# A softmax's sums over keys by one-column products, its output banks added on GpSimd, and a renewed plan, in an attention and state-space kernel

## The chip, the cores and the metric

The kernel runs on one core of one Trainium2 chip, as one program. The metric is the device time of one execution in microseconds (us). Three executions give the time before; a fourth, profiled execution gives the trace. An instruction's engine is named as in the profile: PE is TensorE's matmul, PEld its weight load, DVE is VectorE, ACT is ScalarE, POOL is GpSimd, SP is SyncE, which here only issues DMAs.

## The reference, cut to what matters

A block of a model: layer norm, eight-head cross-attention from 4096 queries to 3202 keys (head width 64), a second layer norm, a state-space scan, and two residual additions, all in float32.

```python
x = _layernorm(builder_state, g1, beta1)          # 4096 x 512
base_n = _layernorm(base_state, g1, beta1)        # 3202 x 512
# _mha: 8 heads of 64
scores = jnp.einsum('bhqd,bhkd->bhqk', q, k) * (1.0 / np.sqrt(HD))
attn = jax.nn.softmax(scores, axis=-1)
out = jnp.einsum('bhqk,bhkd->bhqd', attn, v)
...
x = residual + out @ W_o.T + b_o
xn = _layernorm(x, g2, beta2)
U = (xn @ W_in.T + b_in) @ Bmat
def step(s, u_t):                                 # a scan over the 4096 rows
    s = jax.nn.silu(s @ A.T) + u_t
    return (s, s)
...
return residual + states @ Cmat + mod
```

The change is in the softmax: its denominators (the sums over the keys), the join of the attention output before it is divided by them, and the order in which all pieces of the attention stage stand.

## The kernel before, in words

**Stages.** The first 300 us or so load and normalise the keys and make keys and values in DRAM. The attention stage follows, up to about 2400 us; the state-space scan and the last rows close the program.

**A unit.** The attention is 64 units: one pair of heads (`hp`, four pairs) by 256 queries (`QU`). A unit has 13 steps (`NDC`), each of two chunks of about 123 keys. Keys lie on the partitions, queries along the free axis, so a step's tile is 123 partitions by 2 heads by 2 chunks by 256 queries, 1024 elements to a partition.

- `scores` (L616): eight products of 64x64 weights with 256 columns into a PSUM tile `s` (two buffers).
- `keep` (L630): ACT copies `s` into an SBUF tile `p`. `running` (the pieces `top`, L645): DVE keeps the largest score over the steps; the last step takes three half-size instructions (L639 to L641).
- `spread` (L653), `maximum` (L660), `everywhere` (L668): PE transposes the running maximum, DVE reduces it over the keys, PE spreads the result over the key partitions into the PSUM tile `mb`.
- `subtract` (the pieces `less`, L676): DVE takes the maximum from each kept tile; `weights` (L686): ACT makes the exponentials in place.
- `product` (L705): PE multiplies values by weights into `po`, two PSUM banks, one for each half of the keys. `add` (L694): POOL adds the 13 weight tiles into `acc`, 12 additions of 1024 elements.
- `output` (L735): ACT copies bank 0 of `po` to `o`. `join` (L739): DVE adds bank 1.
- `finish`: `both` (L749), POOL adds the two chunk halves of `acc`, 512 elements; `turn` (L755), PE transposes the result in four pieces into `pd`; `inverse` (L763, L764), DVE sums `pd` over the keys and takes the reciprocal; `wide` (L768), ACT repeats it; `back` (L773), PE transposes it back; `scale` (L781), DVE multiplies `o` by it.

Between these come the pieces of other rows: the next 512 queries' layer norm and heads (`queries`, `heads` L302), and for finished rows the output projection (L902), `x1` (L912), the second layer norm and the scan's inputs (`project`; on POOL `row` L896, `mod` L916 and `factors` L819 to L821).

**Order.** Nothing on the chip picks the order: each engine executes its instructions as written. A class `Plan` writes them. Each piece has an engine, a cost in ns, the pieces it must follow, a due time, and the buffers it takes and gives back. `order` plays the engines forward in time and gives each free engine the ready piece that is due first. `SHIFT` moves the due times of a sort of piece; `LATE` is the delay from a piece's end to the start of one that waits for it; `START` and `AGAIN` are added to the cost of a `scores` or `product` piece on PE, `AGAIN` where the piece before it on PE was one of these too; `RUN` and `ALONE` say how far PE should keep to one of the two kinds. Costs in the plan are of the plan alone: they set an order, not a time. PSUM has one buffer `m` in this stage, which `spread`, `turn`, `back`, the heads, the projection and the transposes take in turn.

Of the kernel before, what the change touches and what calls it, by code (L numbers as in the profile page):

```python
# [10 lines left out]
F32 = mybir.dt.float32  # L11
# [42 lines left out]
class Plan:  # L54
# [7 lines left out]
    LATE = {"PE": 110, "DVE": 130, "ACT": 110, "POOL": 100, "SP": 3000}  # L62
    START, AGAIN = 200, 10
    RUN = 1
    ALONE = dict(scores=300, product=1300)

    SHIFT = {
        "back": -2600, "both": -1300, "everywhere": -2600, "heads": 2000, "heads2": -5800,
        "maximum": 18900, "output": -1300, "product": 1300, "query.copy": -300,
        "query.spread": -3200, "query.turn": 1200, "row.inputs": -1300, "row.mean": 2000,  # L70
        "row.mod": 8100, "row.row": 6500, "row.spread": -1300, "row.turn": 2300, "row.x1": 2600,
        "scores": -300, "spread": 600, "turn": -1900, "weights": 1300,
    }
# [91 lines left out]
def xattn_ssm_kernel(  # L165
# [565 lines left out]
    def output(w):  # L731
        Q, hp, half = w["at"]
        o = op.tile([P, QU], F32, tag="o", name=f"o_{Q}_{hp}_{half}", bufs=12)
        o_t[Q, hp, half] = o
        nc.scalar.copy(o, w["po"][:, 0, :QU])  # L735

    def join(w):
        o = o_t[w["at"]]
        nc.vector.tensor_tensor(o, o, w["po"][:, 1, :QU], ALU.add)  # L739

    def finish(w, i, d, plan):

        name = w["name"]
        at_ = w["at"]

        def both():
            acc = w["acc"]
            w["both"] = accp.tile([CK, 2, QU], F32, tag="both", name=f"both_{name}", bufs=1)
            nc.gpsimd.tensor_tensor(w["both"], acc[:, :, 0, :], acc[:, :, 1, :], ALU.add)  # L749

        def turn():
            w["pd"] = m_tile([P, 2, 2, CK], f"pd_{name}")
            for t in range(2):
                for a in range(2):
                    nc.tensor.transpose(  # L755
                        w["pd"][:, t, a, :],
                        w["both"][:, a, t * P : (t + 1) * P],
                        ident[:CK, :CK],
                    )

        def inverse():
            w["rd"] = small.tile([P, 2, 2], F32, tag="rd", name=f"rd_{name}")
            nc.vector.tensor_reduce(w["rd"], w["pd"], AX.X, ALU.add)  # L763
            nc.vector.reciprocal(w["rd"], w["rd"])  # L764

        def wide():
            w["wide"] = op.tile([P, 2, 2, HD], F32, tag="rd", name=f"wide_{name}", bufs=1)
            nc.scalar.copy(w["wide"], w["rd"].unsqueeze(3).to_broadcast([P, 2, 2, HD]))  # L768

        def back():  # L770
            w["rb"] = m_tile([P, 512], f"rb_{name}")
            for t in range(2):
                nc.tensor.transpose(  # L773
                    w["rb"][:, t * P : (t + 1) * P],
                    w["wide"][:, t].rearrange("p a d -> p (a d)"),
                    ident,
                )

        def scale():
            o = o_t[at_]  # L780
            nc.vector.tensor_tensor(o, o, w["rb"][:, :QU], ALU.mult)  # L781

        plan.add(("both", i), "POOL", 1280, both, [("add", i, NDC - 1)], d - STEP,
                 ["both"], [("acc", ("add", i, 1))])
        plan.add(("turn", i), "PE", 600, turn, [("both", i)], d + 3000,
                 ["m"], [("both", ("both", i))])
        plan.add(("inverse", i), "DVE", 850, inverse, [("turn", i)], d + 5000,
                 ["rd"], [("m", ("turn", i))])
        plan.add(("wide", i), "ACT", 400, wide, [("inverse", i)], d + 6000,
                 ["wide"], [("rd", ("inverse", i))])  # L790
        plan.add(("back", i), "PE", 350, back, [("wide", i)], d + 7000,
                 ["m"], [("wide", ("wide", i))])
        plan.add(("scale", i), "DVE", 390, scale, [("back", i), ("join", i)], d + 8000,
                 [], [("m", ("back", i))])
# [5 lines left out]
    def norm_pieces(plan, k, get, d, after, name, give):  # L800
# [26 lines left out]

        plan.add((*k, "mean"), "ACT", 820, mean_, after, d, ["nm", "xh"])
        plan.add((*k, "spread"), "ACT", 820, spread_, [(*k, "mean")], d + 1000, ["sq"])
        plan.add((*k, "factors"), "POOL", 1050, factors_, [(*k, "spread")], d + 2000,  # L830
# [5 lines left out]
    def queries(plan, Q, d):  # L836

        xns, copied = [], []
        for t in range(NT):
# [12 lines left out]
            def turn(t=t, nv=nv, r=r, v=v):  # L852
                if t % 2 == 0:
# [7 lines left out]
                     ["m", "xn"] if t % 2 == 0 else ["m"], [("xh", (*k, "mean"))])  # L861
            plan.add((*k, "copy"), "ACT", 600, lambda v=v: next(v["turn"], None),
                     [(*k, "turn")], d + 5 * STEP, [], [("m", (*k, "turn"))])
# [5 lines left out]
    def head_pieces(plan, Q, hps, xns, copied, d, apart, xn_):  # L869
        for hp in hps:  # L870
            v = {}

            def head(v=v, hp=hp):
                v["heads"] = heads(Q, hp, xns)
                next(v["heads"])

            plan.add(("heads", Q, hp), "PE", 1850, head, copied, d, ["m", "q"], xn_)
            plan.add(("heads2", Q, hp), "PE", 1850, lambda v=v: next(v["heads"]),
                     [("heads", Q, hp)], d + 1, [], xn_)
            plan.add(("q", Q, hp), "ACT", 680, lambda v=v: next(v["heads"], None),  # L880
                     [("heads2", Q, hp)], d + STEP, [], [("m", ("heads", Q, hp))])
            d += apart

    def project(plan, Q, tiles, d, index):

        for t in tiles:
# [31 lines left out]
            def store(v=v, r=r):  # L918
# [3 lines left out]
            plan.add((*k, "load"), "SP", 60, load, [from_(d - 4 * STEP)], d - 4 * STEP, ["x"])  # L922
            plan.add((*k, "row"), "POOL", 1280, row, [(*k, "load")], d - STEP)
            o_ = [("o_", ("output", i)) for i in units_]
            plan.add((*k, "outs"), "PE", 1850, partial(outs, 0),
# [5 lines left out]
                             ("x1", (*k, "outs")))  # L931
            plan.add((*k, "mod"), "POOL", 1280, mod, [(*k, "x1")], d + 2 * STEP, [],
                     [("x1", (*k, "outs"))])
# [21 lines left out]
            def kept(v=v, hs=hs, c0=c0):  # L955
# [9 lines left out]
                     [("xh", (*k, "mean"))])  # L965
            plan.add((*k, "copy"), "ACT", 600, copy, [(*k, "turn")], d + 6 * STEP, [],
                     [("m", (*k, "turn"))])
# [230 lines left out]
    def last_unit(plan, w, n, d):  # L1198
# [3 lines left out]
        def copied():  # L1202
            o_t[w["at"]] = op.tile([P, QU], F32, tag="o", name=f"o_{w['name']}", bufs=12)
            nc.scalar.copy(o_t[w["at"]], w["po"][:, 0, :QU])

        def summed():
            sums(w["pd"], w["acc"], CK, False, True)
# [13 lines left out]
        plan.add("l.copied", "ACT", 370, copied, [("product", n, NDC - 1)], d, ["o_"])  # L1221
        plan.add("l.join", "DVE", 400, partial(join, w), ["l.copied"], d)
        plan.add("l.summed", "PE", 860, summed,
# [138 lines left out]
    def unit(plan, i):  # L1362
# [20 lines left out]
        for c in range(NDC):  # L1383
# [3 lines left out]
                     [("q", ("heads", Q, hp))], "scores")  # L1387
            plan.add(("keep", i, c), "ACT", 990, partial(keep, w, c), [("scores", i, c)], d + 1000,
                     ["p"], [("s", ("scores", i, c))])
            if c:  # L1390
                plan.add(("top", i, c), "DVE", 1145 if c < NDC - 1 else 2000, partial(running, w, c),
                         [("keep", i, c), ("top" if c > 1 else "keep", i, c - 1)], d + 2000,
# [3 lines left out]
                 [("top", ("top", i, 1))])  # L1396
        plan.add(("maximum", i), "DVE", 665, partial(maximum, w), [("spread", i)], d + 1000,
                 ["max"], [("m", ("spread", i))])
# [3 lines left out]
        for c in range(NDC):  # L1402
            d = (s0 + c + NDC + LAG) * STEP
            plan.add(("less", i, c), "DVE", 1145, partial(subtract, w, c), [("everywhere", i)], d,
                     [], [("b", ("everywhere", i))])
            plan.add(("weights", i, c), "ACT", 1050, partial(weights, w, c), [("less", i, c)],
                     d + 1200)
# [10 lines left out]
            elif c:  # L1418
                plan.add(("add", i, c), "POOL", 2380, partial(add, w, c),
                         [("weights", i, c), ("weights" if c == 1 else "add", i, before)], d + 2400,  # L1420
# [5 lines left out]
        if not w["last"]:  # L1426
            plan.add(("output", i), "ACT", 400, partial(output, w), [("product", i, NDC - 1)], d,
                     ["o_"])
            plan.add(("join", i), "DVE", 400, partial(join, w), [("output", i)], d + 500, [],
                     [("o", ("product", i, 0))])  # L1430
            finish(w, i, d, plan)
# [91 lines left out]
    with tc.manual_schedule():  # L1523
        for g in range(AHEAD):
            load_k(*steps[g])
        plan = Plan(
            dict(
                s=2, m=1, b=1, o=1, p=NDC + LAG + 4, top=2, acc=2, both=1, q=6, x=3, x1=2, xn2=1,
                xn=2, rstd=2, nm=2, sq=2, xh=2, max=2, rd=2, wide=1, o_=12,
# [113 lines left out]
```

## Time and profile before

| what | value |
|---|---|
| median of three runs | 2483.82 us (2482.64 to 2487.72) |
| profiled execution, its own time | 2485.21 us |
| its span in the trace | 2483.4 us |
| granted TensorE clock, mean over the span | 0.993 of full speed |
| busy share of the span: PE, DVE, ACT, POOL | 92%, 85%, 77%, 83% |
| busy in the stretch 500 to 2300 us: PE, DVE, ACT, POOL | 1699.1, 1711.6, 1556.7, 1713.4 us of 1800 |

The shares over the whole span mix the stages: up to 300 us DVE, ACT and POOL have little to do. The stretch from 500 to 2300 us holds nothing but attention units. A group of instructions in the profile is given as line, engine, operation, output and inputs, count, busy time and mean duration, then the idle time of the engine just before these instructions with what ended it. An engine starts its next instruction a little before or after the end of the last, so durations of neighbours overlap or leave gaps; the distance from one start to the next is what an instruction takes up.

### The profile page before, as it was taken

To read this page: it belongs to the slowest core of one execution; us is meant where nothing else is said; L and a number is where in the kernel's file an instruction comes from. 1 tells how busy PE (TensorE), PEld (TensorE's weight loads), DVE (VectorE), ACT (ScalarE), POOL (GpSimd) and SP (SyncE) were. 2 spreads that over 40 slices of the span, in tenths; PEclk is the share of its full clock that TensorE was granted. 3 is DMA by queue.
4 is the path that set the end of the run, shared out by engine and by line. 5 is a ranking of instruction groups with operands and counts; after the bars stand their busy time and mean duration, and the time that the engine had idled before them with its cause. 6 is when DMAs were issued, how large, how long until landed. Compare 5 with 4: busy or idle time off the path is not lost.

```text
span 2483.4 us, 70816 instructions
## 1 busy us (share of the span) xinstructions
PE 2296.9 (92%) x29718; PEld 1355.7 (55%) x29718; DVE 2108.2 (85%) x2307; ACT 1917.3 (77%) x2373; POOL 2071.5 (83%) x1197
## 2 busy tenths in 40 slices
PE   7999888999999999999999999999998999999987
PEld 3444545555555555655565555555565556555544
DVE  2111599999999999999999999999999999999975
ACT  2223588888987899788988988789978998888852
POOL 1111199989998999989998999899999999899984
PEclk9999999999999999999999999999999999999998
DMA  3432322122211222122211221222212221234364
GB/s 119 129 101 82 89 63 61 35 65 66 73 53 55 67 68 69 51 72 78 66 49 51 68 71 54 56 67 75 61 52 66 78 69 51 80 116 124 107 170 149
DMA packets 178140, 190.92 MB, mean 77 GB/s; under 512 B 14252, under 2 KB 151256, under 8 KB 177818
## 3 DMA queue, kind: packets, MB, share of 16 engines
q1 hardware_dynamic: 173270, 178.67, 24.3%
q10 hardware_dynamic: 4548, 7.67, 1.0%
q8 instruction: 237, 3.88, 0.7%
q14 instruction: 85, 0.70, 0.1%
HBM read 156.40 MB, written 29.89 MB: 75 GB/s over the span
## 4 chain that ended last, share of the span: by engine, by line
PE 44%; DVE 21%; POOL 13%; issue 10%; ACT 8%; DMA 2%; SPq 1%; ACTq 0%; POOLq 0%; DVEq 0%
PE s L616 13%; PE po L705 12%; POOL acc L694 12%; DVE top L645 12%; DVE p L676 6%; PE pq L302 5%; ACT p L630 4%; ACT p L686 3%; PE pv L543 3%; PE pk L569 3%; PE pa L902 1%; PE mb L668 1%; PE tt L653 1%; PE pd L755 1%; DMA x<-in_x_dram 1%
## 5 line engine op out<-in xcount | busy, mean ns | idle before, releaser
L694 POOL TENSOR_TENSOR acc<-p,acc 122x1024 f32<-122x1024 f32 x701 | 1660.3, 2369 | 64.1 <-ACT p L686 26.2
L676 DVE TENSOR_TENSOR p<-p,mb 123x1024 f32<-123x1024 f32 (+2 forms) x832 | 996.2, 1210 | 27.8 <-PE mb L668 27.8
L630 ACT COPY p<-s 123x1024 f32<-123x1024 f32 (+2 forms) x832 | 837.0, 1009 | 206.8 <-PE s L616 178.6
L616 PE MATMUL s<-q,k 64*64 64x256 f32 (+3 forms) x13312 | 884.9, 384 | 90.9 <-DVE top L645 79.9
L686 ACT ACTIVATE p<-p 123x1024 f32<-123x1024 f32 (+2 forms) x832 | 874.8, 1061 | 80.8 <-DVE p L676 77.3
L705 PE MATMUL po<-p,v 64*64 64x256 f32 (+3 forms) x13312 | 857.3, 379 | 26.9 <-ACT p L686 25.1
L645 DVE TENSOR_TENSOR top<-s,top 123x1024 f32<-123x1024 f32 (+1 forms) x640 | 777.4, 1215 | 11.8 <-ACT p L630 11.3
L616 PEld LDWEIGHTS s<-q,k 64*64 64x64 f32 (+3 forms) x13312 | 448.2, 130 | 428.6 <-DVE top L645 154.5
L705 PEld LDWEIGHTS po<-p,v 64*64 64x64 f32 (+3 forms) x13312 | 489.8, 133 | 268.4 <-ACT p L686 70.0
L694 POOL TENSOR_TENSOR acc<-p,p 124x1024 f32<-124x1024 f32 x64 | 152.3, 2380 | 94.2 <-DMA k<-kd 73.0
L242 POOL TENSOR_SCALAR ve_c<-mv_c 123x1 f32<-123x1 f32 (+2 forms) x26 | 6.0, 232 | 147.7 <-DVE mv_c L235 118.6
L302 PE MATMUL pq<-xn,wq 128*128 128x256 f32 x512 | 127.2, 392 | 0.0
L902 PE MATMUL pa<-wo,o 128*128 128x512 f32 x240 | 119.0, 618 | 0.0
L513 DVE COPY ct<-tp_c 128x492 f32<-128x492 f32 (+2 forms) x13 | 8.7, 671 | 125.1 <-PE tp_c L270 125.1
L302 PEld LDWEIGHTS pq<-xn,wq 128*128 128x128 f32 x512 | 92.2, 189 | 34.3 <-issue 23.6
L577 ACT ACTIVATE ks<-pk,bias 128x492 f32<-128x492 f32 (+3 forms) x28 | 18.0, 643 | 120.0 <-PE pk L569 58.1
L645 DVE TENSOR_TENSOR top<-s,p 124x1024 f32<-124x1024 f32 x64 | 78.0, 1219 | 37.8 <-DMA k<-kd 31.8
L543 PE MATMUL pv<-wv,ct 128*123 128x512 f32 (+2 forms) x208 | 98.8, 620 | 0.0
L660 DVE TENSOR_REDUCE m<-tt 128x4 f32<-128x496 f32 x64 | 42.9, 671 | 58.8 <-PE tt L653 58.8
L569 PE MATMUL pk<-ct,wk 128*128 128x492 f32 (+3 forms) x224 | 89.1, 550 | 0.0
L749 POOL TENSOR_TENSOR both<-acc 124x512 f32<-124x512 f32 x63 | 81.2, 1289 | 2.0
L902 PEld LDWEIGHTS pa<-wo,o 128*128 128x128 f32 x240 | 40.6, 189 | 51.9 <-issue 50.8
(196 smaller groups left out, 1514.3 us busy)
## 6 DMA issues: line engine op xcount, KB each, us to landing
k<-kd SPq DMA_DIRECT2D x324, 123.0 KB
v<-vd SPq DMA_DIRECT2D x324, 123.0 KB
k<-kd SPq DMA_DIRECT2D x108, 124.0 KB
v<-vd SPq DMA_DIRECT2D x108, 124.0 KB
xr<-in_x_dram SPq DMA_DIRECT2D x32, 256.0 KB
x1d<-xr SPq DMA_DIRECT2D x32, 256.0 KB
x<-in_x_dram SPq DMA_DIRECT2D x28, 256.0 KB
cx<-in_ctx_dram SPq DMA_DIRECT2D x18, 246.0 KB
```

The costliest lines, as they stand in the source:

```text
L302: nc.tensor.matmul(pq[:, half * QU : (half + 1) * QU], wq[:, i, hp * P : (hp + 1) * P], xns[half][:, i, :], start=(i == 0), stop=(i == NC ...
L543: nc.tensor.matmul(pv[:n, :H], ct[:, i, o : o + n], wv[:, i, :], start=(i == 0), stop=(i == NC - 1),)
L569: nc.tensor.matmul(pk[:, :n_g], wk[:, i, hp * P : (hp + 1) * P], ct[:, i, :n_g], start=(i == 0), stop=(i == NC - 1),)
L616: nc.tensor.matmul(s[k0:k1, a, b, :], kts[(*w["at"][:2], c)][r, b * n + k0 : b * n + k1], q[r], start=True, stop=True, skip_group_check=True,)
L630: nc.scalar.copy(t[:n], w["ps"][c][:n])
L645: nc.vector.tensor_tensor(w["top"][:n], s[:n], before[:n], ALU.max)
L676: nc.vector.tensor_tensor(t[:n], t[:n], w["mb"][:n].unsqueeze(2).to_broadcast([n, 2, 2, QU]), ALU.subtract,)
L686: nc.scalar.activation(t[:n], t[:n], AF.Exp)
L694: nc.gpsimd.tensor_tensor(w["acc"][:n], t[:n], before[:n], ALU.add)
L705: nc.tensor.matmul(w["po"][a * HD : (a + 1) * HD, k, :QU], vts[(*w["at"][:2], c)][k0:k1, b, a * HD : (a + 1) * HD], t[k0:k1, a, b, :], sta ...
L749: nc.gpsimd.tensor_tensor(w["both"], acc[:, :, 0, :], acc[:, :, 1, :], ALU.add)
L902: nc.tensor.matmul(v["pa"], o_t[Q, c, t // 2][:, t % 2 * P : (t % 2 + 1) * P], wo[:, c, :], start=(c == 0), stop=(c == NC - 1),)
```

## The change

1. **Sums over keys.** `both` goes. `turn` no longer transposes: 16 products take a quarter of `acc` (124 keys by 64 queries) as weights and one column of ones as the moving operand, and add up in PSUM over the two chunks, so that the sums over the keys lie in `pd`, 128 queries by 2 by 2. Queries 0 to 63 and 64 to 127 of a tile go to the two column halves of the array in turn. `inverse` is then the reciprocal alone.
2. **Join.** `output` copies both banks of `po` to an SBUF tile `two` (one buffer); `join` adds the two halves on POOL and makes `o`. `po` is given back by `output`, not by `join`. The program's very last unit keeps its way (`joined`, on DVE).
3. **Plan.** New costs for most pieces, new `SHIFT`, `START` 200 to 130, `AGAIN` 10 to 35, `RUN` 1 to 4, `ALONE` of scores 300 to 600. So the order on every engine is a new one.

```diff
-    START, AGAIN = 200, 10
-    RUN = 1
-    ALONE = dict(scores=300, product=1300)
+    START, AGAIN = 130, 35
+    RUN = 4
+    ALONE = dict(scores=600, product=1300)
...
     def output(w):
         Q, hp, half = w["at"]
+        w["two"] = accp.tile([P, 2, QU], F32, tag="two", name=f"two_{w['name']}", bufs=1)
+        nc.scalar.copy(w["two"], w["po"][:, :, :QU])
+
+    def join(w):
+        Q, hp, half = w["at"]
         o = op.tile([P, QU], F32, tag="o", name=f"o_{Q}_{hp}_{half}", bufs=12)
         o_t[Q, hp, half] = o
-        nc.scalar.copy(o, w["po"][:, 0, :QU])
-
-    def join(w):
-        o = o_t[w["at"]]
-        nc.vector.tensor_tensor(o, o, w["po"][:, 1, :QU], ALU.add)
+        nc.gpsimd.tensor_tensor(o, w["two"][:, 0, :], w["two"][:, 1, :], ALU.add)
...
-        def both():
-            acc = w["acc"]
-            w["both"] = accp.tile([CK, 2, QU], F32, tag="both", name=f"both_{name}", bufs=1)
-            nc.gpsimd.tensor_tensor(w["both"], acc[:, :, 0, :], acc[:, :, 1, :], ALU.add)
-
         def turn():
-            w["pd"] = m_tile([P, 2, 2, CK], f"pd_{name}")
-            for t in range(2):
-                for a in range(2):
-                    nc.tensor.transpose(
-                        w["pd"][:, t, a, :],
-                        w["both"][:, a, t * P : (t + 1) * P],
-                        ident[:CK, :CK],
+            w["pd"] = m_tile([P, 2, 2], f"pd_{name}")
+            for k, (b, t, a) in enumerate((b, t, a) for b in range(2) for t in range(2) for a in range(2)):
+                for h in range(2):
+                    q = t * P + h * HD
+                    nc.tensor.matmul(
+                        w["pd"][h * HD : (h + 1) * HD, t, a : a + 1],
+                        w["acc"][:, a, b, q : q + HD],
+                        ones[:CK, 0:1],
+                        start=(k == 0),
+                        stop=(k == 7),
+                        skip_group_check=True,
                     )
 
         def inverse():
             w["rd"] = small.tile([P, 2, 2], F32, tag="rd", name=f"rd_{name}")
-            nc.vector.tensor_reduce(w["rd"], w["pd"], AX.X, ALU.add)
-            nc.vector.reciprocal(w["rd"], w["rd"])
+            nc.vector.reciprocal(w["rd"], w["pd"])
...
-        plan.add(("both", i), "POOL", 1280, both, [("add", i, NDC - 1)], d - STEP,
-                 ["both"], [("acc", ("add", i, 1))])
-        plan.add(("turn", i), "PE", 600, turn, [("both", i)], d + 3000,
-                 ["m"], [("both", ("both", i))])
-        plan.add(("inverse", i), "DVE", 850, inverse, [("turn", i)], d + 5000,
+        plan.add(("turn", i), "PE", 1150, turn, [("add", i, NDC - 1)], d + 1000,
+                 ["m"], [("acc", ("add", i, 1))])
+        plan.add(("inverse", i), "DVE", 180, inverse, [("turn", i)], d + 5000,
                  ["rd"], [("m", ("turn", i))])
...
-                plan.add(("top", i, c), "DVE", 1145 if c < NDC - 1 else 2000, partial(running, w, c),
+                plan.add(("top", i, c), "DVE", 1128 if c < NDC - 1 else 2055, partial(running, w, c),
...
-        plan.add(("maximum", i), "DVE", 665, partial(maximum, w), [("spread", i)], d + 1000,
+        plan.add(("maximum", i), "DVE", 595, partial(maximum, w), [("spread", i)], d + 1000,
...
-                plan.add(("add", i, c), "POOL", 2380, partial(add, w, c),
+                plan.add(("add", i, c), "POOL", 2346, partial(add, w, c),
...
-            plan.add(("output", i), "ACT", 400, partial(output, w), [("product", i, NDC - 1)], d,
-                     ["o_"])
-            plan.add(("join", i), "DVE", 400, partial(join, w), [("output", i)], d + 500, [],
-                     [("o", ("product", i, 0))])
+            plan.add(("output", i), "ACT", 480, partial(output, w), [("product", i, NDC - 1)], d,
+                     ["two"], [("o", ("product", i, 0))])
+            plan.add(("join", i), "POOL", 750, partial(join, w), [("output", i)], d + 500, ["o_"],
+                     [("two", ("output", i))])
```

## The prediction

> **What bounds the kernel now.** I read the page first, then the busy times of the stretch from 500 to 2300 us, which holds nothing but attention units, then the waits of each engine in that stretch, then the timeline at one turn from unit to unit.
>
> The page has no engine over 92%, but that mixes stages; its slices and its costliest groups show POOL full from 300 us on:
>
> ```profile
> POOL 1111199989998999989998999899999999899984
> ...
> L694 POOL TENSOR_TENSOR acc<-p,acc 122x1024 f32<-122x1024 f32 x701 | 1660.3, 2369 | 64.1 <-ACT p L686 26.2
> ...
> L749 POOL TENSOR_TENSOR both<-acc 124x512 f32<-124x512 f32 x63 | 81.2, 1289 | 2.0
> ```
>
> How long a unit takes is read from a row that comes once in a unit (four instructions each, 63 units), with its first and last start:
>
> ```profile
> L755 PE MATMUL pd<-ident,both x252: 269/269/330, 330.2 to 2399.1; 124*128 124x124 f32 x126
> ```
>
> (2399.1 - 330.2) / 62 = 33.37 us; the 1800 us stretch holds 54 units, 33.33 us each. Its busy times (PE, PEld, DVE, ACT, POOL):
>
> ```profile
> 500.00:2300.00 1800.00, 1699.09 (x24388) 1031.20 (x24380) 1711.64 (x1761) 1556.65 (x1882) 1713.39 (x916) 1.00 0.23 68
> ```
>
> PE, DVE and POOL are all at 94 to 95%. Which of them sets the pace is told by what they wait for in that stretch (total us, times, longest):
>
> ```profile
> POOL acc L694 <- ACT p L686: 39.8, 48, 2.4
> ```
>
> ```profile
> DVE m L660 <- PE tt L653: 52.9, 32, 3.9
> DVE p L676 <- PE mb L668: 18.8, 21, 1.0
> ```
>
> ```profile
> PE s L616 <- DVE top L645: 60.6, 93, 1.4
> ```
>
> POOL waits 41 us in 54 units (these 39.8 and 1.2 for a DMA), 0.76 us a unit; the rest of its idle time are gaps between neighbours. So its work takes up (1800 - 41) / 54 = 32.57 us of 33.33. DVE waits 81.9 us (these two, and 10.2 for ACT's copies), 1.52 a unit: 31.82 us taken up. PE is busy 31.46 us a unit, and its largest wait, 1.12 us a unit, is for DVE to give back a score buffer. ACT has 14% to spare. So POOL's load is the floor, and what lies on top is DVE's stall at the turn of a unit, which starves ACT and then POOL. The timeline shows that turn, and the parts to be changed:
>
> ```profile
> 1213.75 14.57 POOL L694 TENSOR_TENSOR acc<-p,acc 123x1024 f32<-123x1024 f32 x6
> ...
> 1215.55 0.69 DVE L641 TENSOR_TENSOR top<-s,top 124x512 f32<-124x512 f32 x1
> ...
> 1216.38 0.62 PE L653 MATMUL tt<-ident,top 124*128 124x124 f32 x4 [1.07 <-DVE top L641]
> ...
> 1217.04 0.68 DVE L660 TENSOR_REDUCE m<-tt 128x4 f32<-128x496 f32 x1 [0.80 <-PE tt L653]
> ...
> 1217.95 0.65 PE L668 MATMUL mb<-ident,m 128*124 128x128 f32 x4
> ...
> 1218.64 1.22 DVE L676 TENSOR_TENSOR p<-p,mb 124x1024 f32<-124x1024 f32 x1 [0.93 <-PE mb L668]
> ...
> 1224.21 0.36 ACT L735 COPY o<-po 128x256 f32<-128x256 f32 x1
> ...
> 1225.43 0.41 DVE L739 TENSOR_TENSOR o<-o,po 128x256 f32<-128x256 f32 x1
> ...
> 1225.76 1.22 DVE L676 TENSOR_TENSOR p<-p,mb 123x1024 f32<-123x1024 f32 x1
> ...
> 1228.28 2.38 POOL L694 TENSOR_TENSOR acc<-p,p 124x1024 f32<-124x1024 f32 x1
> ...
> 1230.61 1.30 POOL L749 TENSOR_TENSOR both<-acc 124x512 f32<-124x512 f32 x1
> ...
> 1231.85 4.82 POOL L694 TENSOR_TENSOR acc<-p,acc 122x1024 f32<-122x1024 f32 x2
> ...
> 1232.64 0.67 DVE L763 TENSOR_REDUCE rd<-pd 128x4 f32<-128x496 f32 x1
> ...
> 1233.35 0.18 DVE L764 RECIPROCAL rd<-rd 128x4 f32<-128x4 f32 x1
> ```
>
> At 1216 us the maximum waits for PE's transposes, which wait for the last running maximum: DVE idles 0.80, then 0.93 us until `mb` is there. Further down: 6 additions in 14.57, 2.43 us each; the copied output ready at 1224.6; `both` only at 1230.61.
>
> **The change, part by part.** Distances from start to start are used, per unit, against 33.33.
>
> *POOL.* `both` leaves: 1230.61 to 1231.85, 1.24 us. `join` comes, 256 elements with both inputs in SBUF; no row has that size. By the line through 512 elements (1.24) and 1024 (1228.28 to 1230.61, 2.33) it is 0.70; at worst it costs what `both` did, 1.24. A rule speaks against it: GPSIMD Engine Reference, Engine selection, puts elementwise work with two inputs on VectorE, about twice as fast. The rows agree in kind (0.41 us long on DVE), and twice that, 0.82, would make POOL's floor 32.15; I take the line, as both its ends are POOL's own rows. 32.57 - 1.24 + 0.70 = 32.03.
>
> *DVE.* The sum in `inverse` leaves (1232.64 to 1233.35, 0.71), and `join` (1225.43 to 1225.76, 0.33). The reciprocal and `scale` stay. 31.82 - 1.04 = 30.78. Beside the load, the order: in the built program before, the maximum stands directly behind the three last-step instructions in 29 of 64 units, and `less` directly behind the maximum in 26. In the changed program it is 3 and none: another `less` or `top` of 1.13 us stands between, about as long as the 0.80 and 0.93 us to be covered. Most of the 52.9 + 18.8 us, 1.33 a unit, should go. So DVE comes to about 31 us and stops pacing.
>
> *PE.* Four transposes leave (0.57 to the next piece: 1231.96 to 1232.53). 16 float32 products come, two records each, so 32 weight loads of 64 columns with one column moving. Two rows bound them. Loads of this size with one moving column into the same column half, in the preparation:
>
> ```profile
> 117.23 0.54 PEld L447 LDWEIGHTS pb<-bi,bm 128*64 128x64 f32 x8 [0.16 <-issue]
> ```
>
> (0.54 - 0.14) / 7 = 57 ns from one to the next; 32 of them 1.83 us. Loads that alternate between the column halves, in the last unit's sums:
>
> ```profile
> 2407.56 0.20 PEld L723 LDWEIGHTS pd<-p,ones 123*64 123x64 f32 x4
> ```
>
> Four loads within 0.20 us, less 0.14 for one: they go in pairs, 0.06 us a pair, 16 pairs 0.93 us. The change alternates halves, so the second row is nearer; with some 0.15 us to drain I take 1.1. Here a rule speaks against the change: TensorE: Matmul & The Clock Gate, The mechanism (of packing small matmuls), says that a load overlaps running matmuls only where the row groups differ, and all 16 have the same rows; its section on LDWEIGHTS makes 64 / 1.2 = 53 ns of a load, so 1.7 us alone. The row with alternate halves shows loads side by side in spite of equal rows, so I go with it and keep 1.83 as the upper end. PE's busy time becomes 31.46 - 0.57 + 1.1 = 32.0, and of its waits, 1.81 a unit in all, I leave about a third, 0.65: those for `mb`, for the transposes and the first exponentials, not those for DVE's backlog. With X for the price of the products PE's period is 31.54 + X: 32.64 at 1.1.
>
> *ACT.* The copy of two banks instead of one: 128x256 from PSUM takes 0.37 us, 128x512 (the copies of transposed rows) 0.57 to 0.59: 0.21 more. Behind it on ACT wait `keep` and `weights`; ACT waits 135.5 us in the stretch for scores, 2.5 a unit, and that hides it. Without the cover it is 0.21 x 62 = 13 us.
>
> *New waits.* `join` waits on POOL for ACT's copy, with additions queued behind it. The built order puts it behind the unit's last addition, sometimes behind the first one or two of the next; in the timeline the copy is done 6 us before that point. `turn` now waits on PE for the last addition, with the next scores and products behind it; before, the same place waited for `both`, 1.3 us later. `po` comes back one DVE instruction earlier, `two` has a whole unit's time to come free. All count nothing. SP issues the same 1267 DMAs, the loads of keys and values with the scores and products as before.
>
> *The plan.* Its costs for DVE and POOL now equal the starts in the trace (DVE 1128, POOL 2346 plus its 100 of delay against 2.43 us measured); before, they were 1 to 2% too long. That is worth nothing by itself; the order is counted above.
>
> *Sum.* Floors: POOL 32.03, PE 32.64 with its waits, DVE 31. Three engines so close never meet the highest floor exactly, but PE's figure already holds waits. Period 32.65, 0.68 less, x 62 = 42 us. The 330 us before and 84 us after the units are unchanged. Against the profiled execution (span 2483.4, own time 2485.2) that makes 2443; the median of the runs is 1.4 us lower, so 2442.
>
> **The rivals.**
>
> *Small gain (chance 0.20).* POOL keeps the pace: `join` costs nearly 1.24, or starvation stays since ACT's exponentials come no sooner. Then the floor is 32.57 with some 0.5 of waits, 33.07: 16 us, 2468. For it: 2.43 us additions leave POOL no other slack, and half of POOL's waits could come from PE's placement. Against: two busy engines are relieved at once.
>
> *Slower (0.12).* The one-column products take the PE: loads one after the other, as the row of 57 ns has them, with a drain on either side[...]: X = 2.1. PE's period is then 33.64, 0.31 x 62 = 19 us more, 2503. It decides from X = 1.8 up. For it: PE is already busy 94%, and the rule above. Against: the alternate halves.
>
> *No change (0.03).* New stalls of the new order eat the gain, 2484. Also that the change doesn't do what it says is here: an order written from costs that miss PE.
>
> *The likeliest (0.65)*: 2442, with its own range 2422 to 2463: X from 0.93 to 1.4 gives 2431 to 2460, the rest is for the waits that I left on PE.
>
> **How the numbers follow.** The runs before lie within 0.2%, 5 us; less than that can't be told from no change. The range 2422 to 2480 holds the likeliest case but its lowest corner, and the small gain; left out are the slower cases and a fuller gain (period 32.3), about 2 in 10. Faster by over 0.2%: 0.65 + 0.20 = 0.85; within: 0.03; slower: 0.12.
>
> **What would show it.** In the profile after: the products' 32 loads within about 1 us of PEld a unit; `join` near 0.75 us on POOL; DVE's waits for `tt` and `mb` below 20 us in all; the once-a-unit row at 32.6 us; POOL's waits for ACT no larger. The prediction is wrong if PE's busy share comes to 98% or more, if scores wait for PE's own `turn`, or if POOL still waits 0.7 us a unit with its load lighter.

## The result, and the profile after

The changed kernel takes 2449.53 us (median of four runs, 2443.13 to 2453.52), the kernel before 2483.94 beside it: a ratio of 0.9854, 95% interval 0.9842 to 0.9866. That is 34 us less; 42 were forecast, 2442 us. The profiled execution took 2451.61 us.

The page after, its span, busy shares, slices and the groups that answer to those shown of before (lines have moved by one or two):

```profile
span 2449.8 us, 74218 instructions
...
PE 2332.0 (95%) x31482; PEld 1395.8 (57%) x31482; DVE 2049.7 (84%) x2181; ACT 1920.1 (78%) x2373; POOL 2036.2 (83%) x1197
...
PE   7999899999999999999999999999999999999987
...
DVE  2121599999999998999999999999899989999964
...
POOL 1111199989999999999999999999999999999983
...
L695 POOL TENSOR_TENSOR acc<-p,acc 122x1024 f32<-122x1024 f32 x701 | 1660.0, 2368 | 52.0 <-ACT p L687 11.1
...
L687 ACT ACTIVATE p<-p 123x1024 f32<-123x1024 f32 (+2 forms) x832 | 874.7, 1061 | 118.5 <-DVE p L677 113.3
...
L617 PE MATMUL s<-q,k 64*64 64x256 f32 (+3 forms) x13312 | 870.7, 382 | 26.8 <-DVE top L646 18.0
...
L661 DVE TENSOR_REDUCE m<-tt 128x4 f32<-128x496 f32 x64 | 42.9, 670 | 36.8 <-PE tt L654 36.8
```

The same rows of before, as far as they were not shown:

```profile
PE   7999888999999999999999999999998999999987
...
L616 PE MATMUL s<-q,k 64*64 64x256 f32 (+3 forms) x13312 | 884.9, 384 | 90.9 <-DVE top L645 79.9
...
L686 ACT ACTIVATE p<-p 123x1024 f32<-123x1024 f32 (+2 forms) x832 | 874.8, 1061 | 80.8 <-DVE p L676 77.3
```

From 310 us on, PE's slices are at 9 through the attention stage; before, two of them at its start and one later were at 8. Scores (L617) wait less for VectorE to give back their buffers, 18.0 us against 79.9, and ACT's exponentials (L687) wait longer for VectorE's `less`, 113.3 us against 77.3. The row that comes once in a unit, with first and last start, and the stretch of attention units (PE, PEld, DVE, ACT, POOL):

```profile
L754 PE MATMUL pd<-ones,acc x2016: 196/197/218, 327.1 to 2359.3; 124*64 124x1 f32 x184
```

```profile
500.00:2300.00 1800.00, 1754.43 (x26278) 1076.33 (x26266) 1685.60 (x1679) 1582.47 (x1912) 1711.33 (x932) 1.00 0.24 70
```

(2359.3 - 327.1) / 62 = 32.78 us a unit, against 33.37; 0.59 x 62 = 37 us, so the whole gain lies in the units; the profiled executions differ by 33.6, and the rest of the program gave 3 us back. The stretch now holds 1800 / 32.78 = 54.9 units. The waits in it, of VectorE, GpSimd and PE (total us, times, longest):

```profile
DVE top L646 <- ACT p L631: 67.2, 37, 3.4
DVE m L661 <- PE tt L654: 36.8, 28, 2.7
DVE s L640 <- ACT p L631: 4.2, 20, 0.3
DVE o L782 <- PE rb L774: 0.9, 6, 0.2
```

```profile
POOL acc L695 <- ACT p L687: 35.3, 24, 2.7
```

```profile
PE po L706 <- ACT p L687: 14.4, 47, 0.6
PE s L617 <- DVE top L646: 12.9, 35, 1.3
PE po L706 <- ACT two L735: 7.9, 16, 0.9
```

VectorE waits 109 us, not less than the 82 of before but more: the wait for `mb` is gone from the stretch, that for `tt` fell from 52.9 to 36.8, and a new one stands on top, 67.2 us at the first running maximum of a unit, for ACT's copy of the scores. PE's wait for score buffers fell from 60.6 to 12.9 us. The new places of the change:

```profile
L754 PEld LDWEIGHTS pd<-ones,acc 124*64 124x64 f32 x2016 | 63.9, 138 | 26.8 <-POOL acc L695 15.2 <-issue 11.2 <-POOL o L741 0.4
L741 POOL TENSOR_TENSOR o<-two 128x256 f32<-128x256 f32 x63 | 46.4, 736 | 0.7 <-ACT two L735 0.7
...
L735 ACT COPY two<-po 128x512 f32<-128x512 f32 x63 | 37.1, 590 | 7.9 <-PE po L706 7.9
```

### The profile page after: what moved, and what is told of

It reads as the page before. It is cut to its first block, busy times and chain, and to the rows that moved or that the text cites. A ratio compares the mean times of both kernels' runs of the same rounds, so it can differ in the third digit from the quotient of the medians.

```text
span 2449.8 us, 74218 instructions
## 1 busy us (share of the span) xinstructions
PE 2332.0 (95%) x31482; PEld 1395.8 (57%) x31482; DVE 2049.7 (84%) x2181; ACT 1920.1 (78%) x2373; POOL 2036.2 (83%) x1197
## 4 chain that ended last, share of the span: by engine, by line
PE 44%; DVE 18%; ACT 13%; POOL 12%; issue 10%; DMA 2%; SPq 1%; ACTq 0%; POOLq 0%; DVEq 0%
PE s L617 13%; PE po L706 11%; POOL acc L695 10%; DVE top L646 10%; ACT p L631 6%; ACT p L687 5%; PE pq L303 4%; DVE p L677 4%; PE pv L544 3%; PE pk L570 3%; PE pa L901 2%; PE pd L754 1%; PE mb L669 1%; PE tt L654 1%; DVE top L641 1%
## 5 line engine op out<-in xcount | busy, mean ns | idle before, releaser
L687 ACT ACTIVATE p<-p 123x1024 f32<-123x1024 f32 (+2 forms) x832 | 874.7, 1061 | 118.5 <-DVE p L677 113.3
L706 PE MATMUL po<-p,v 64*64 64x256 f32 (+3 forms) x13312 | 868.4, 382 | 36.2 <-ACT p L687 26.1
L617 PE MATMUL s<-q,k 64*64 64x256 f32 (+3 forms) x13312 | 870.7, 382 | 26.8 <-DVE top L646 18.0
L706 PEld LDWEIGHTS po<-p,v 64*64 64x64 f32 (+3 forms) x13312 | 480.8, 133 | 298.3 <-ACT p L687 82.7
L617 PEld LDWEIGHTS s<-q,k 64*64 64x64 f32 (+3 forms) x13312 | 454.7, 131 | 333.6 <-DVE top L646 75.6
L754 PEld LDWEIGHTS pd<-ones,acc 124*64 124x64 f32 x2016 | 63.9, 138 | 26.8 <-POOL acc L695 15.2
L661 DVE TENSOR_REDUCE m<-tt 128x4 f32<-128x496 f32 x64 | 42.9, 670 | 36.8 <-PE tt L654 36.8
L754 PE MATMUL pd<-ones,acc 124*64 124x1 f32 x2016 | 69.3, 198 | 2.1 <-POOL acc L695 2.1
```

What stands on the lines that cost most here:

```text
L617: nc.tensor.matmul(s[k0:k1, a, b, :], kts[(*w["at"][:2], c)][r, b * n + k0 : b * n + k1], q[r], start=True, stop=True, skip_group_check=True,)
L687: nc.scalar.activation(t[:n], t[:n], AF.Exp)
L706: nc.tensor.matmul(w["po"][a * HD : (a + 1) * HD, k, :QU], vts[(*w["at"][:2], c)][k0:k1, b, a * HD : (a + 1) * HD], t[k0:k1, a, b, :], sta ...
L754: nc.tensor.matmul(w["pd"][h * HD : (h + 1) * HD, t, a : a + 1], w["acc"][:, a, b, q : q + HD], ones[:CK, 0:1], start=(k == 0), stop=(k == 7),
```

## The experiments

Twelve kernels ran, each beside the kernel before. Three theories stand against one another. The *load theory* is the forecast's: the loads that leave GpSimd and VectorE make the gain, wherever they leave. The *order theory*: the new order makes it, whatever the loads. The *fit theory* came up after the first eight runs: an order and the loads for which it was written pay only together.

| kernel | median us | ratio to before, 95% interval |
|---|---|---|
| the change | 2449.5 | 0.9854 (0.9842 to 0.9866) |
| e1 plan alone | 2495.6 | 1.0042 (1.0027 to 1.0056) |
| e2 rewrites, old plan | 2510.6 | 1.0102 (1.0083 to 1.0120) |
| e3 sums alone, old plan | 2511.3 | 1.0110 (1.0092 to 1.0128) |
| e4 join alone, old plan | 2554.4 | 1.0284 (1.0267 to 1.0301) |
| e9 rewrites in the order of before | 2496.4 | 1.0047 (1.0030 to 1.0064) |
| e10 sums in the order of before | 2498.3 | 1.0059 (1.0041 to 1.0076) |
| e5 change, loads one after the other | 2489.0 | 1.0004 (0.9990 to 1.0018) |
| e6 change, more GpSimd work | 2467.3 | 0.9923 (0.9905 to 0.9941) |
| e11 change, more VectorE work, PSUM | 2494.2 | 1.0044 (1.0029 to 1.0059) |
| e12 change, more VectorE work, SBUF | 2505.9 | 1.0093 (1.0068 to 1.0119) |
| e7 change, more VectorE work, early | 2530.6 | 1.0172 (1.0155 to 1.0189) |
| e8 change, join issued on VectorE | 2530.5 | 1.0181 (1.0159 to 1.0202) |

### The parts, each with a plan of its own

**e1, the plan alone.** Sums and join are those of before, with the costs that the new plan would give them; `both` keeps its shift.

```diff
-        plan.add(("turn", i), "PE", 1150, turn, [("add", i, NDC - 1)], d + 1000,
+        plan.add(("both", i), "POOL", 1240, both, [("add", i, NDC - 1)], d - STEP,
...
+        plan.add(("turn", i), "PE", 600, turn, [("both", i)], d + 3000,
...
+            plan.add(("output", i), "ACT", 295, partial(output, w), [("product", i, NDC - 1)], d,
...
+            plan.add(("join", i), "DVE", 330, partial(join, w), [("output", i)], d + 500, [],
```

> The renewed plan alone: new costs, SHIFT, START, AGAIN, RUN and ALONE, with sums and join as before (both on GpSimd, transposes, reduction, join on VectorE). Load theory (the loads that leave GpSimd and VectorE make the gain, the order only closes VectorE's stalls at the turn of a unit): GpSimd's 32.57 us a unit stays the floor, with 0.5 us of waits 33.07 us, 2468 us. Order theory (the new order makes nearly all of the gain): 2450 us. If the order is worth nothing without the loads: 2484 us.

2495.6 us, slower than before by 10. The new numbers of the plan are not worth 34 us, nor the 16 of the load theory, by themselves: on the old pieces they lose. VectorE's waits for `tt` and `mb` did fall there, to 29.6 and 3.9 us in the stretch, and 56.9 us for ACT's copies came in their place.

**e2, both rewrites with the plan of before.** The changed kernel with the old `START`, `AGAIN`, `RUN`, `ALONE`, `SHIFT` and costs.

```diff
-    START, AGAIN = 130, 35
-    RUN = 4
+    START, AGAIN = 200, 10
+    RUN = 1
...
-                plan.add(("add", i, c), "POOL", 2346, partial(add, w, c),
+                plan.add(("add", i, c), "POOL", 2380, partial(add, w, c),
```

> Both rewrites (sums by one-column products, join on GpSimd) with the plan's numbers of before; only the three new pieces have the costs of the change. The maximum stands directly behind the last-step instructions in 20 of 64 units, less directly behind the maximum in 32. Load theory: GpSimd at 32.0 us a unit, VectorE's stalls half there, 32.85 us, 2454 us. Order theory: 2480 us.

2510.6 us, slower by 25, where the load theory had 2454. The loads are gone (VectorE's and GpSimd's busy times in the stretch fall to 1643.7 and 1663.7 us) and the time with them is longer. Load theory and order theory both miss.

**e3 and e4, one rewrite each with the plan of before.** e3 has the new sums and VectorE's join; e4 the old sums and GpSimd's join. Both are e2 with one part undone:

```diff
e3:
-        nc.gpsimd.tensor_tensor(o, w["two"][:, 0, :], w["two"][:, 1, :], ALU.add)
+        nc.vector.tensor_tensor(o, o, w["po"][:, 1, :QU], ALU.add)
e4:
+            nc.gpsimd.tensor_tensor(w["both"], acc[:, :, 0, :], acc[:, :, 1, :], ALU.add)
...
+            nc.vector.tensor_reduce(w["rd"], w["pd"], AX.X, ALU.add)
```

> Sums by one-column products alone, join on VectorE and the plan as before. GpSimd loses 1.24 us a unit and gets nothing back (31.3 us), VectorE loses 0.71, PE gains 0.45. Load theory: GpSimd no longer sets the pace, PE with its waits does: 32.65 us, 2442 us, as good as the whole change or better. Order theory: 2480 us.

> The join alone on GpSimd, sums and plan as before. GpSimd gets 0.70 us a unit more (33.27), VectorE loses 0.33. Load theory: GpSimd's load is the floor, so slower: 33.27 and 0.3 of waits, 33.6 us, 2500 us. If GpSimd's load were not the floor, VectorE's relief would show: 2470 us.

e3: 2511.3 us instead of 2442. GpSimd has the lightest load of these four and starves; its largest wait in the stretch, 39.8 us before, is

```profile
POOL acc L694 <- ACT p L686: 123.2, 63, 13.0
```

e4: 2554.4 us instead of 2500. That it is slower fits the load theory, but the surplus is 1.1 us a unit where the added load is 0.70, and VectorE, which was relieved, waits most:

```profile
DVE top L645 <- ACT p L630: 75.7, 44, 4.2
DVE m L660 <- PE tt L653: 43.9, 26, 3.8
```

In all four kernels the plan wrote a new order on every engine, so loads and order moved together. The next two hold the order still.

### The rewrites in the order of before

**e9 and e10.** The plan plans the old pieces at the old costs; only what a piece issues is new. `both` issues nothing, `turn` the 16 products, `inverse` the reciprocal; in e9 also `output` copies both banks and `join` adds on GpSimd, in the places of the old pieces.

```diff
         def both():
-            acc = w["acc"]
...
+            pass
...
         plan.add(("both", i), "POOL", 1280, both, [("add", i, NDC - 1)], d - STEP,
```

> Both rewrites in the order of before: the plan keeps its old pieces, costs and places, and only the instructions that a piece issues are those of the change (the piece both issues nothing). VectorE loses 1.04 us a unit, GpSimd 0.54, PE gains 0.45, and the 29 and 26 bad places at the turn stay. Load theory: most of the gain is here, 2460 us. Fit theory (loads pay only in an order written for them): 2484 us or slower. Forecast of the record: 2454 us, as for the rewrites with the old plan.

> The same with the sums alone: join on VectorE as before, in the order of before. GpSimd loses 1.24 us a unit, VectorE 0.71, PE gains 0.45. Load theory: GpSimd free, PE paces: 2455 us. If PE's load is what counts in this order: 62 x 0.45 x 0.7 (the price of PE time from the serial loads) = 20 us slower, 2505 us.

2496.4 and 2498.3 us, 12 and 14 slower than before. With the order held, the rewrites bring nothing in all; the load theory falls, and the join adds little either way. What the relief of GpSimd and VectorE is worth by itself in this order is not shown, since the products also load PE by 0.44 us a unit more. Of e10's forecasts the one that counts PE's load alone, 20 us slower, is the nearest to the 14. VectorE's waits in e9 show where its relief went:

```profile
DVE m L660 <- PE tt L653: 56.4, 32, 4.1
DVE o L784 <- PE rb L776: 24.9, 32, 1.5
DVE top L645 <- ACT p L630: 22.9, 53, 1.3
DVE p L676 <- PE mb L668: 18.3, 21, 0.9
DVE rd L767 <- PE pd L756: 10.2, 18, 0.8
```

The two that hold `scale` (`o` for `rb`) and the reciprocal (`rd` for `pd`) were under 1 us together in the stretch of before. VectorE now comes to these instructions before PE's results are there, so what it was relieved of turns in part into waiting. In all it waits 135 us there, 82 before.

### What a microsecond more costs in the changed kernel

These keep the changed kernel's plan and so its order, and add work to one engine.

**e5, PE.** The products in another sequence, all of one column half first:

```diff
-            for k, (b, t, a) in enumerate((b, t, a) for b in range(2) for t in range(2) for a in range(2)):
-                for h in range(2):
+            for h in range(2):
+                for k, (b, t, a) in enumerate((b, t, a) for b in range(2) for t in range(2) for a in range(2)):
```

> The changed kernel, with the same order of pieces on every engine; only the 16 one-column products of a unit stand otherwise: first all eight for queries 0 to 63 of a tile, then all eight for 64 to 127, so neighbours load the same column half. By the row of 57 ns the 32 loads take 1.83 us instead of 0.93. If PE sets the pace now (PE period 31.54 + X): 0.9 us a unit more, 62 x 0.9 = 56 us, 2505 us. If GpSimd sets it and PE has slack: under 20 us, 2465 us. If loads of the two halves never ran side by side, the time is that of the change, 2450 us.

The loads of one unit, in the changed kernel and in e5 (timeline of PE's weight loads: start, us):

```profile
1245.41 1.01 PEld L754 LDWEIGHTS pd<-ones,acc 124*64 124x64 f32 x32 [0.39 <-issue]
```

```profile
1226.51 1.73 PEld L754 LDWEIGHTS pd<-ones,acc 124*64 124x64 f32 x32 [0.38 <-issue]
```

1.73 us instead of 1.01, and 2489.0 us, 39.5 more than the change: 39.5 / (63 x 0.72) = 0.87 us for each us on PE. VectorE's wait for ACT's copies of the scores rose from 67.2 to 93.3 us in the stretch.

**e6, GpSimd.** A second addition behind each join.

```diff
         nc.gpsimd.tensor_tensor(o, w["two"][:, 0, :], w["two"][:, 1, :], ALU.add)
+        dum = accp.tile([P, QU], F32, tag="dum", name=f"dum_{w['name']}", bufs=1)
+        nc.gpsimd.tensor_tensor(dum, w["two"][:, 0, :], w["two"][:, 1, :], ALU.add)
```

> The changed kernel and its order, with a second addition of 128x256 on GpSimd behind each join, into a tile that nobody reads: 0.70 us a unit more on GpSimd (32.7 us). If GpSimd's load is the floor: 0.6 us a unit, 37 us, 2487 us. If PE sets the pace and GpSimd has slack: under 10 us, 2458 us.

2467.3 us, 17.8 more: 17.8 / (63 x 0.70) = 0.40 for each us. Neither forecast; GpSimd's wait for ACT's exponentials gave way by half, from 35.3 to

```profile
POOL acc L695 <- ACT p L687: 18.9, 27, 2.0
```

**e11, VectorE.** Two multiplications more ahead of `scale`, one input in PSUM.

```diff
             o = o_t[at_]
+            dum = accp.tile([P, QU], F32, tag="dum", name=f"dum_{name}", bufs=1)
+            nc.vector.tensor_tensor(dum, o, w["rb"][:, :QU], ALU.mult)
+            nc.vector.tensor_tensor(dum, o, w["rb"][:, :QU], ALU.mult)
```

> The changed kernel and its order, with two extra multiplications of 128x256 on VectorE ahead of each scale, one input in SBUF and one in PSUM, into a tile that nobody reads: 0.66 us a unit more on VectorE, nearly what its reduction took. If VectorE's slack is real (2 us of waits a unit): under 10 us, 2455 us. If VectorE's load sets the pace: 41 us, 2490 us. If any extra instruction there costs what the one in e7 did: 2530 us.

2494.2 us, 44.7 more. The expectation put the two at 0.33 us each, as their kind takes up between other neighbours; here they take up 0.45 each, 1234.94 to 1235.84 for both:

```profile
1234.94 0.41 DVE L783 TENSOR_TENSOR dum<-o,rb 128x256 f32<-128x256 f32 x1
1235.39 0.42 DVE L784 TENSOR_TENSOR dum<-o,rb 128x256 f32<-128x256 f32 x1
1235.84 0.42 DVE L785 TENSOR_TENSOR o<-o,rb 128x256 f32<-128x256 f32 x1
```

So 63 x 0.90 = 56.7 us were added, and each costs 44.7 / 56.7 = 0.79 us. VectorE has little slack, although it waits 2.0 us a unit. Its two large waits in e11 are nearly those of the change (67.2 and 36.8 us); PE's wait for score buffers is not, it rose from 12.9 to 38.5:

```profile
DVE top L646 <- ACT p L631: 64.5, 36, 3.3
DVE m L661 <- PE tt L654: 36.6, 28, 2.7
```

```profile
PE s L617 <- DVE top L646: 38.5, 72, 1.6
```

The three prices compare kernels that ran at different times. Taken through the ratios to before they are 0.82 (PE), 0.39 (GpSimd) and 0.82 (VectorE), each uncertain by about 0.1: PE's and VectorE's can't be told apart, GpSimd's is about half of theirs.

Waits that added work does not shorten are no slack. Here they stand at the turn of a unit, for PE; between two turns VectorE hardly waits. The timeline of the changed kernel shows one turn:

```profile
1224.26 0.69 DVE L642 TENSOR_TENSOR top<-s,top 124x512 f32<-124x512 f32 x1
...
1224.87 1.21 DVE L677 TENSOR_TENSOR p<-p,mb 124x1024 f32<-124x1024 f32 x1
...
1226.31 1.95 PE L617 MATMUL s<-q,k 64*64 64x256 f32 x32
1227.52 1.93 ACT L631 COPY p<-s 124x1024 f32<-124x1024 f32 x2 [0.35 <-PE s L617]
...
1228.57 1.23 DVE L646 TENSOR_TENSOR top<-s,p 124x1024 f32<-124x1024 f32 x1 [2.49 <-ACT p L631]
```

The score buffers come back with the last-step instruction (begun at 1224.26); PE is in a heads piece and begins the next two scores at 1226.31; ACT copies them from 1227.52; VectorE begins the first running maximum at 1228.57, after 2.49 us of waiting. VectorE, PE and ACT stand here as links of one loop through two score buffers: with more work on PE, VectorE waits longer (e5), and with more on VectorE, PE does (e11). That would explain that VectorE's and PE's microsecond both cost most of one; no run changed the number of buffers.

**e7, e8 and e12, VectorE with both inputs in SBUF.** e7 puts GpSimd's extra addition of e6 on VectorE; e8 issues the join itself there; e12 stands where e11 does, once, with `o` by `o`.

```diff
e7:
+        nc.vector.tensor_tensor(dum, w["two"][:, 0, :], w["two"][:, 1, :], ALU.add)
e8:
-        nc.gpsimd.tensor_tensor(o, w["two"][:, 0, :], w["two"][:, 1, :], ALU.add)
+        nc.vector.tensor_tensor(o, w["two"][:, 0, :], w["two"][:, 1, :], ALU.add)
e12:
+            nc.vector.tensor_tensor(dum, o, o, ALU.mult)
```

> The changed kernel and its order, with an extra addition of 128x256 on VectorE behind each copy of the output banks, into a tile that nobody reads: about 0.33 us a unit more on VectorE. If VectorE has about 2 us of slack now, as forecast: nothing, 2450 us. If it still sets the pace: 0.33 x 62 = 20 us, 2470 us.

> The changed kernel and its order (the plan still books the join on GpSimd), but the join's instruction is issued on VectorE, in the place that the plan gave it: GpSimd loses 0.70 us a unit (31.3 us), VectorE gets 0.33. If GpSimd's load sets the pace: 0.5 us a unit less, 2419 us. If PE does: no change within 5 us, 2450 us. If VectorE does: 2465 us.

> The same with one extra multiplication only, but both inputs in SBUF: 0.33 us a unit if it runs as those with an input in PSUM do. In e7 such an instruction took 1.23 us on average, up to 2.65, while GpSimd added. Port theory (two SBUF inputs wait for GpSimd's running instruction): about 1.2 us a unit more on VectorE whatever the place, 2500 to 2530 us, and single durations up to 2.7 us. Place theory (e7 stood in a bad place): under 10 us, 2455 us.

2530.6, 2530.5 and 2505.9 us: 81, 81 and 56 more than the change, for a single short instruction a unit. e7 and e8 so measured something else than they were made for. The durations of that instruction (minimum, median, maximum in ns) in e7 and e12, and of e11's two with one input in PSUM:

```profile
L743 DVE TENSOR_TENSOR dum<-two x63: 411/670/2651, 331.3 to 2438.5; 128x256 f32<-128x256 f32 x63
```

```profile
L783 DVE TENSOR_TENSOR dum<-o x63: 410/760/2489, 331.9 to 2423.2; 128x256 f32<-128x256 f32 x63
```

```profile
L783 DVE TENSOR_TENSOR dum<-o,rb x63: 407/411/422, 332.6 to 2411.4; 128x256 f32<-128x256 f32 x63
L784 DVE TENSOR_TENSOR dum<-o,rb x63: 420/421/423, 333.1 to 2411.8; 128x256 f32<-128x256 f32 x63
```

The same size and type takes 0.41 us with an input in PSUM, every time, and 0.41 to 2.65 us with both in SBUF, 1.23 on average in e7, 1.37 in e8, 0.96 in e12. One of e7's in the timeline, behind GpSimd's join:

```profile
1233.19 0.74 POOL L741 TENSOR_TENSOR o<-two 128x256 f32<-128x256 f32 x1
1233.88 2.37 POOL L695 TENSOR_TENSOR acc<-p,acc 124x1024 f32<-124x1024 f32 x1
1234.08 2.45 DVE L743 TENSOR_TENSOR dum<-two 128x256 f32<-128x256 f32 x1
```

VectorE's instruction starts while GpSimd adds and ends 0.28 us after that addition's end (1236.25). This is the rule of the three traces: all 144 of these instructions that took over 0.5 us started while a GpSimd instruction ran, and ended 0.28 to 0.29 us after it. Of the 45 shorter ones 35 started with GpSimd idle and 10 near the end of its instruction. The place theory for e12 falls.

At VectorE's price e12's sum comes out: from its start to that of `scale` the instruction takes up 1.06 us on average, 63 x 1.06 x 0.79 = 53 us of 56. For e7 it is 63 x 1.15 x 0.79 = 57 of 81 (the mean less 0.08 us, which neighbours overlap), for e8 63 x 1.29 x 0.79 = 64 less GpSimd's 63 x 0.70 x 0.40 = 18, so 46 of 81. The other 24 and 35 us stay open. The instruction stands elsewhere in the unit there than in e11 and e12, and no run tells what that place costs.

## Why the prediction was right or wrong

The time, its range and its sign held, at 34 us of the 42. Most of its steps held too; the reason that joined them did not.

- *GpSimd's load.* `join` was put at 0.70 us from start to start; it takes up 0.69 (1233.19 to 1233.88 in e7's lines) and is 0.74 long. (1800 - 41.1) / 54.9 = 32.0 us taken up, 32.03 forecast. Right.
- *GpSimd's waits.* They are 41.1 / 54.9 = 0.75 us a unit, as before (0.76). "POOL still waits 0.7 us a unit with its load lighter" was one of the forecast's own signs of being wrong, and it came, though the sum itself left 0.62 for these waits (32.65 less 32.03). With a price of 0.40 for its microsecond (e6), GpSimd's load alone doesn't set the pace after the change.
- *The products' price.* 1.1 us was taken, 0.93 for the loads and some 0.15 to drain. The loads take 1.01, and from their start to that of the next piece on PE it is 1.03 in the unit shown: nearly the right sum, with the loads a little longer and hardly any drain. The Trainium skill's TensorE: Matmul & The Clock Gate (The mechanism) says that a load overlaps running matmuls only where the row groups differ; an estimate from that page's section LDWEIGHTS (columns / 1.2 ns, 53 ns for 64) makes 1.7 us of the 32. In e5, where neighbours load the same half, they take 1.73; with alternate halves 1.01, on the same rows. So the 1.7 is the price of one column half, and the row chosen was the right one.
- *PE.* Busy 1754.4 / 54.9 = 32.0 us, as forecast; waits 41.8 / 54.9 = 0.76 instead of 0.65. 32.7 against a measured 32.78. In its parts the 0.65 was partly luck: it was left for `mb`, the transposes and the first exponentials, and of the 41.8 us these have 16.8; score buffers, which were to be free, have 13.9 and the copy of the output 7.9.
- *ACT and the new waits.* The copy of two banks takes 0.59 us. `join` waited 0.7 us in all. One wait put at nothing exists: the first product of a unit waits for that copy, 7.9 us in the stretch. The traces list 1204 DMA issues of SP in both kernels, where the forecast has 1267; that they are the same holds.
- *VectorE's load.* 30.78 us forecast; (1800 - 109.1) / 54.9 = 30.8. Right.
- *VectorE's stall: wrong.* "Most of the 52.9 + 18.8 us, 1.33 a unit, should go"; in the profile after, below 20 us was to be seen. `mb` went, `tt` stayed at 36.8. The order did change as forecast: the maximum stands directly behind the last-step instructions in 3 units. But in 36 units PE has two score pieces directly ahead of the transposes, which start 1.9 us after the first of these, and one `less` of 1.13 us does not always cover that; these units have 23 us of the wait. And 67.2 us for ACT's copies came. What stood next in line, the first scores of the new unit behind a heads piece, was not named.
- *"So DVE comes to about 31 us and stops pacing": wrong.* e11 shows a price of 0.79, no lower than PE's as far as the runs can tell. The step that failed is the equation of wait with slack: that an engine with 2 us of waits a unit has 2 us to give.
- *"That is worth nothing by itself", of the plan, and the gain as a matter of loads: wrong.* e9 gives the loads without the order, 12 us slower; e2 the loads with the old numbers, 25 slower, 2454 expected; e1 the new numbers with the old pieces, 10 slower. Only the pair gained. That the forecast's sum came near is in part luck: PE's formula happened to describe the order that the new numbers wrote for the new loads; from before's trace it could not be known that another order with the same loads is 61 us (e2) or 47 us (e9) longer.

Rivals: PE's serial loads, the slower rival, decided from X = 1.8 in the forecast; e5, at 0.72 above the change, is just level with before (1.0004). That size was right. The small gain, with GpSimd keeping the pace, did not come: 34 us against its 16, and e6's price is 0.40. The rival of no change named an order that eats the gain at a chance of 0.03; the six kernels with only a part of the change, with the old numbers or in the old order were all slower than before, so an order can do that. What chance that deserved for the change itself, they do not tell.

What stays open: why this order fits these loads, and which of the plan's numbers matters. The runs changed them all at once (e1, e2), and no run tells `SHIFT` from `RUN` or from the costs. Nor was the change's order run with the old loads, nor the old order with lighter GpSimd and VectorE alone. And each set of numbers wrote one order only, so how far the times of such orders scatter by chance is not known; that the new numbers suit the new loads, and did not just hit upon a good order, is not shown.

## What to carry to other kernels

Where four engines are each over 85% busy in a stage and their order is written out, treat a rewrite and the order for it as one change: plan its pieces anew with their own costs before measuring it, and do not judge it by a run in the old order alone. An engine's idle time is no measure of its slack; add a known piece of work to it in the same order and see what the total does (here about 0.8, 0.9 and 0.4 us for each us on VectorE, PE and GpSimd). Read from the trace what the added piece takes up: here 0.45 us, where 0.33 were expected. And keep one input of a VectorE instruction in PSUM while GpSimd is busy.

## What the runs showed of the hardware

A VectorE instruction with two inputs in SBUF waits for the GpSimd instruction that is running: 0.41 us became up to 2.65, next to GpSimd additions of 2.37, and all 144 that took over 0.5 us ended 0.28 to 0.29 us after GpSimd's, where one with an input in PSUM kept 0.41 to 0.42 in all 126 cases. The Trainium skill, SBUF — State Buffer, SBUF: two separate sides, says that the two engines lock a port pair for a whole instruction and that VectorE's need of it with two SBUF inputs holds against GpSimd instructions that read SBUF; the runs agree, and give the price. It was not in the forecast, and it matters for the change: once both banks are copied to SBUF, the join has two SBUF inputs, and on VectorE it took 1.37 us on average (e8), not 0.41. The rule of the skill's GPSIMD Engine Reference (Engine selection), cited in the forecast, puts such an addition on VectorE, as GpSimd takes about twice as long. The lengths agree where nothing stands in the way, 0.41 us against 0.74; with GpSimd busy the choice is the other way round here: e8 is 81 us slower than the change.

One-column products with 64 columns of weights on the same rows: the 32 loads of a unit took 1.01 us with the two column halves in turn and 1.73 us with neighbours in the same half (e5).
